# Loop tables copied by ScalarE at the outset, the small steps of three batch norm chunks moved to GpSimd, ten rooms for fetched images

## The chip, the cores and the metric

The kernel runs on one core of a Trainium2 chip. Its time is the device time of one execution in microseconds (us). The core has five engines that run their own instruction queues and wait for each other through semaphores: TensorE (PE, matrix products), VectorE (DVE), ScalarE (ACT), GpSimd (POOL) and SyncE (SP, which here only issues DMA transfers). Within a queue, instructions start in the order in which they stand.

## The reference

The input x has 128 images of 128 channels of 16x16 pixels. The reference does two layers.

```python
x = x + _L0_conv_ref(_gn(x), ...)            # group norm, batch norm, 4-bit activations, conv, batch norm, conv
t = _to_tokens(x)
t = t + _L1_attn_ref(_ln_t(t), ...)          # two Mamba-like scans, forward and backward
t = t + _L1_ffn_ref(_ln_t(t), ...)           # top-2 of 8 experts
x = _from_tokens(t, x)
```

What matters here is the first layer. The group norm takes the mean and variance of each image over groups of 4 channels; the batch norm takes the mean and variance of each channel over all 128 images of what the group norm returned. So nothing can be convolved before the last image has been read:

```python
def _bn(x, gamma, beta):
    m = jnp.mean(x, axis=(0, 2, 3), keepdims=True)
    v = jnp.var(x, axis=(0, 2, 3), keepdims=True)
    return (x - m) * jax.lax.rsqrt(v + EPS) * gamma[None, :, None, None] + beta[None, :, None, None]

h = _act_quant(_bn(x, gamma1, beta1))
out = _conv3x3(h, _weight_quant(w1) * pat1)
out = _act_quant(_bn(out, gamma2, beta2))
out = _conv3x3(out, _weight_quant(w2) * pat2) + x
```

## The kernel before

Channels lie on the 128 partitions; two images (128x512 values) are the unit of work, 64 units in all. There are four stages.

**Outset.** SP issues the 64 loads of the units (`xr`, line 371), then some 40 loads of the weights of the second layer (`load_weights`, lines 278 to 307), then the load of the second conv's weights (`w2`, line 401). DVE takes mean and variance of most images with `bn_stats` (line 443); every fourth image, up to `cuts[3]`, is summed by ACT in two passes, `Copy` (line 441) and `Square` (line 457). The images are worked in four chunks of 48, 48, 24 and 8. After the sums of a chunk come its small steps, on arrays of 128 partitions by as many columns as the chunk has images: mean and variance from the two halves, the mean over 4 channels by a matrix product with `grp`, the same for the variance, `1/sqrt`, one Newton step, and the products that the batch norm needs (`normed`, lines 420 to 434). Before the change `1/sqrt` is a `Sqrt` on ACT (line 481) and a reciprocal on DVE (line 424), and nearly all the small steps are DVE's, placed between its `bn_stats`. Between them DVE and ACT also prepare the first conv's weights (`conv_weights`, lines 148 to 185). At the end DVE folds the four chunks into a scale and an offset for each image (lines 495 to 511: `sc1`, `bi1`).

The outset also builds two constant tables for the main loop, `rows0` and `cols0` (128x2048 in bf16 each): POOL copies them together in `patterns` (lines 376 to 397), from two small selectors `heads` and `triple` that POOL also builds (lines 94 to 108), and SP stores them to HBM (`rows_d`, `cols_d`, lines 489 and 490), from where the main loop's `constants` loads them. Before the change these two stores stand last in SP's queue, behind the weight loads.

**First conv.** For each unit: ACT or POOL applies scale and offset (`q`, lines 525 and 527), DVE quantises into a padded buffer (`hpad`, line 192), PE does five products (`cv`, line 218), ACT adds an offset and copies the result out (`o1`, line 541), DVE takes its statistics (line 542), SP stores it to HBM (line 544), except for the first 8 units, which are kept (`kept`). The buffers of this stage lie where the outset's had been (the pool `setup1`), so its first instructions also wait until those buffers are free.

**Second conv.** For each unit: SP fetches the stored unit (`fetch`, line 618), ACT applies the second batch norm (line 622), DVE quantises, PE convolves, POOL or ACT scales x (lines 663 and 665), DVE adds (line 666), PE transposes (`yt_ps`, line 631), ACT copies it out (`yt`, line 633), SP stores it (`y_d`, line 635). Fetched units have 6 buffers, and the program asks for unit i+5 at unit i. The order in which the instructions of all these stages stand in the five queues is set by a scheduler when the kernel is built, from its own estimate of durations.

**Main loop** (from about 294 us on). The second layer, 64 units in an order written out by hand (`T`, a table of places, `manual_schedule`). It holds most of the time and the change does not touch it.

GpSimd's power instruction is used for `1/sqrt` in several places already: lines 133 (1 column), 557 (1), 595 (4) and 1060 (8), where `mhalf` holds -0.5.

Of the kernel before, what the change touches and what calls it, by code (L numbers as in the profile page):

```python
# [8 lines left out]
F32 = mybir.dt.float32  # L9
BF16 = mybir.dt.bfloat16  # L10
AF = mybir.ActivationFunctionType
ALU = mybir.AluOpType
AX = mybir.AxisListType

P = 128
NT = 256
EPS = 1e-5
# [4 lines left out]
NH = 4  # L22
HD = 64
# [11 lines left out]
def kernel(ctx: ExitStack, tc: tile.TileContext, a: dict):  # L35

    nc = tc.nc
    x_d, out_d = a["x"], a["out"]
    B = x_d.shape[0]
    NP = B // 2  # L40
# [19 lines left out]
    rows_d = dram.tile([P, NH, 2, 2, P], BF16, name="rows_d")  # L60
    cols_d = dram.tile([P, 2, 2, 2, 2, P], BF16, name="cols_d")

    ident = const.tile([P, P], F32, name="ident")
    make_identity(nc, ident)
    ones = const.tile([P, P], F32, name="ones")
# [30 lines left out]
    nc.gpsimd.memset(heads, 0.0)  # L96
    nc.gpsimd.memset(triple, 0.0)
    for m in range(2):
        for q in range(3):
            for t in (3 + 4 * q, 15 + 4 * q):  # L100
                nc.gpsimd.affine_select(
                    out=heads, in_=heads, pattern=[[-1, NH]], compare_op=ALU.not_equal,
                    fill=-1.0, base=-(64 + 32 * m + t), channel_multiplier=1,
                )
            nc.gpsimd.affine_select(
                out=triple[:, m : m + 1], in_=triple[:, m : m + 1], pattern=[[0, 1]], compare_op=ALU.not_equal,
                fill=1.0, base=-(64 + 32 * m + q), channel_multiplier=1,
            )
# [235 lines left out]
    with tc.tile_pool(name="w1p", bufs=1) as w1p:  # L344

        grp = w1p.tile([P, P], F32, name="grp")
        nc.gpsimd.affine_select(
            out=grp, in_=ones, pattern=[[-4, 32], [0, 4]], compare_op=ALU.is_ge, fill=0.0,
            base=0, channel_multiplier=1,
        )  # L350
        nc.gpsimd.affine_select(
            out=grp, in_=grp, pattern=[[4, 32], [0, 4]], compare_op=ALU.is_ge, fill=0.0,
            base=3, channel_multiplier=-1,
        )
        nc.vector.tensor_scalar(grp, grp, 0.25, None, ALU.mult)
# [4 lines left out]
        with tc.tile_pool(name="setup1", bufs=1) as setup, tc.tile_pool(  # L360
            name="psa", bufs=1, space=PSUM
        ) as psa:
            w1 = w1p.tile([P, 9, P], F32, name="w1", tag="w")
# [5 lines left out]

            for i in range(NP):  # L370
                nc.sync.dma_start(xr[i], x_c[:, 2 * i : 2 * i + 2, :])
            rows0 = setup.tile([P, NH, 2, 2, P], BF16, name="rows0")
            cols0 = setup.tile([P, 2, 2, 2, 2, P], BF16, name="cols0")
            far = setup.tile([HD, 1], BF16, name="far")

            def patterns():
                nc.gpsimd.memset(far, -1e30)
                for h in range(NH):
                    nc.gpsimd.tensor_copy(
                        rows0[:, h].rearrange("p d t l -> p (d t l)"), heads[:, h : h + 1].to_broadcast([P, 4 * P])  # L380
                    )
                    nc.gpsimd.tensor_copy(
                        rows0[0:HD, h].rearrange("p d t (f l) -> p (d t f) l", l=HD),
                        ident[0:HD, 0:HD].unsqueeze(1).to_broadcast([HD, 2 * 2 * 2, HD]),
                    )
                for m in range(2):
                    for d in range(2):
                        sign = 1 - 2 * d
                        nc.gpsimd.tensor_copy(
                            cols0[:, m, d].rearrange("p j f l -> p (j f l)"), triple[:, m : m + 1].to_broadcast([P, 4 * P])  # L390
                        )
                        for half in range(2):
                            nc.gpsimd.affine_select(
                                out=cols0[0:HD, m, d, :, half, :], in_=far.unsqueeze(2).to_broadcast([HD, 2, P]),
                                pattern=[[0, 2], [sign, P]], compare_op=ALU.is_ge, fill=0.0,
                                base=-sign * HD * half - 1, channel_multiplier=-sign,
                            )

            load_weights()
            w2 = w1p.tile([P, 9, P], F32, name="w2", tag="w")  # L400
            nc.sync.dma_start(w2, a["L0_conv_w2"])

# [11 lines left out]
            cuts = [0, 3 * B // 8, 3 * B // 4, B - max(B // 16, 1), B]  # L414
# [5 lines left out]
            def normed(c):  # L420

                of = slice(cuts[c], cuts[c + 1])
                var_, gm_, dev_, ga_, qv_, dm_ = (t[:, of] for t in (var, gm, dev, ga, qv, dm))
                nc.vector.reciprocal(ga_, ga_)
                nc.vector.tensor_tensor(dm_, ga_, ga_, ALU.mult)
                nc.vector.tensor_tensor(dm_, dm_, qv_, ALU.mult)
                nc.vector.tensor_scalar(dm_, dm_, -0.5, 1.5, ALU.mult, ALU.add)
                nc.vector.tensor_tensor(ga_, ga_, dm_, ALU.mult)
                nc.vector.scalar_tensor_tensor(shift[:, of], gm_, -1.0, ga_, ALU.mult, ALU.mult)
                nc.gpsimd.tensor_scalar(ares[:, of], ga_, 1.0, SCALE, ALU.add, ALU.mult)  # L430
                nc.gpsimd.tensor_scalar(bres[:, of], shift[:, of], SCALE, None, ALU.mult)
                nc.vector.tensor_tensor(dev_, dev_, ga_, ALU.mult)
                nc.vector.tensor_tensor(var_, var_, ga_, ALU.mult)
                nc.vector.tensor_tensor(var_, var_, ga_, ALU.mult)

            for c in range(4):
                of = slice(cuts[c], cuts[c + 1])
                for b in range(B)[of]:
                    x_b = xr[b // 2][:, b % 2, :]
                    if by_scalar(b):  # L440
                        nc.scalar.activation(junk, x_b, AF.Copy, accum_out=bst[:, b, 1:2])
                    else:
                        behind = nc.vector.bn_stats(bst[:, b, :], x_b)
                if c > 0:

                    with tc.issue_after(behind.ins):
                        normed(c - 1)
                mean_, var_, dm_, gm_, dev_, qv_, ga_ = (t[:, of] for t in (mean, var, dm, gm, dev, qv, ga))
                mine = [b for b in range(B)[of] if by_scalar(b)]
                if mine:  # L450

                    picked = slice(mine[0], cuts[c + 1], 4)
                    nc.vector.tensor_scalar(neg[:, picked], bst[:, picked, 1], -1.0 / NT, None, ALU.mult)
                    nc.vector.tensor_scalar(bst[:, picked, 1], neg[:, picked], -1.0, None, ALU.mult)
                    nc.vector.tensor_scalar(bst[:, picked, 4], neg[:, picked], -1.0, None, ALU.mult)
                    for b in mine:
                        nc.scalar.activation(
                            junk, xr[b // 2][:, b % 2, :], AF.Square, bias=neg[:, b : b + 1],
                            accum_out=bst[:, b, 2:3],
                        )  # L460

                nc.vector.tensor_tensor(mean_, bst[:, of, 1], bst[:, of, 4], ALU.add)
                nc.vector.tensor_scalar(mean_, mean_, 0.5, None, ALU.mult)
                nc.vector.tensor_tensor(dm_, bst[:, of, 1], bst[:, of, 4], ALU.subtract)
                nc.vector.tensor_tensor(dm_, dm_, dm_, ALU.mult)
                nc.vector.tensor_tensor(var_, bst[:, of, 2], bst[:, of, 5], ALU.add)
                nc.vector.tensor_scalar(dm_, dm_, 0.25, None, ALU.mult)
                nc.vector.scalar_tensor_tensor(var_, var_, 1.0 / NT, dm_, ALU.mult, ALU.add)
# [4 lines left out]
                nc.vector.tensor_copy(gm_, gm_ps)  # L473
                nc.vector.tensor_tensor(dev_, mean_, gm_, ALU.subtract)
                nc.vector.tensor_tensor(qv_, dev_, dev_, ALU.mult)
                nc.vector.tensor_tensor(qv_, qv_, var_, ALU.add)
# [3 lines left out]
                nc.vector.tensor_scalar(qv_, gv_ps, EPS, None, ALU.add)  # L480
                nc.scalar.activation(ga_, qv_, AF.Sqrt)
# [3 lines left out]
                if c == 1:  # L485
                    for _ in weights:
                        pass
                    patterns()
                    nc.sync.dma_start(rows_d, rows0)
                    nc.sync.dma_start(cols_d, cols0)  # L490
                if c == 3:
                    normed(c)
# [112 lines left out]
    def conv2(taps, nq):  # L605
        with tc.tile_pool(name="pc", bufs=6) as pc, tc.tile_pool(
# [8 lines left out]
            def fetch(i):  # L615
                if NP > i and i not in kept:
                    qs[i] = pc.tile([P, 2, NT], F32, name=f"q2_{i}", tag="q")
                    nc.sync.dma_start(qs[i], o1_d[i])
# [30 lines left out]
            for i in range(5):  # L649
                fetch(i)  # L650
            for i in range(3):
                quantised(i)
            for i in range(NP):
                b = 2 * i
                fetch(i + 5)
# [656 lines left out]
```

## Time and profile before

| | us |
|---|---|
| median of 3 runs (2553.06 to 2555.53) | 2554.39 |
| the profiled execution, its own time | 2554.94 |
| its span, first to last instruction | 2553.1 |
| last unit of x issued by SP | 51.4 |
| scale and offset of the first conv ready (`bi1`) | 77.6 |
| first `q` of the first conv on ACT | 85.7 |
| first product of the first conv on PE | 87.3 |
| first product of the second conv on PE | 174.7 |
| last `xr` sum of the second conv on DVE | 292.2 |

| engine | busy us | share of the span |
|---|---|---|
| PE | 2415.3 | 95% |
| DVE | 2253.2 | 88% |
| ACT | 2173.0 | 85% |
| POOL | 1629.3 | 64% |

The shares are means over all four stages. The change lies in the first 294 us, so the rows to read are those of that stretch: there PE is idle for the first 87 us, POOL is nearly idle from 20 to 87 us, and DVE is busy 98% of the time from 20 to 60 us.

### The profile page before, as it was taken

To read this page: it belongs to the slowest core of one execution; us is meant where nothing else is said; L and a number is where in the kernel's file an instruction comes from. 1 tells how busy PE (TensorE), PEld (TensorE's weight loads), DVE (VectorE), ACT (ScalarE), POOL (GpSimd) and SP (SyncE) were. 2 spreads that over 40 slices of the span, in tenths; PEclk is the share of its full clock that TensorE was granted. 3 is DMA by queue.
4 is the path that set the end of the run, shared out by engine and by line. 5 is a ranking of instruction groups with operands and counts; after the bars stand their busy time and mean duration, and the time that the engine had idled before them with its cause. 6 is when DMAs were issued, how large, how long until landed. Compare 5 with 4: busy or idle time off the path is not lost.

```text
span 2553.1 us, 49290 instructions
## 1 busy us (share of the span) xinstructions
PE 2415.3 (95%) x15940; PEld 1479.9 (58%) x15940; DVE 2253.2 (88%) x6163; ACT 2173.0 (85%) x4455; POOL 1629.3 (64%) x1694
## 2 busy tenths in 40 slices
PE   0688889999999999999999999999999999999997
PEld 0235456666666666666666666666666666666663
DVE  8787699999999999999999999999999999999883
ACT  5678699888889998889898888998988899898881
POOL 3468026676666666666666666666667666666666
PEclk9999899999999999999999999999999999999998
DMA  9358633434444444444444344444433443443343
GB/s 287 124 192 281 227 67 110 125 111 123 130 124 122 122 125 118 120 132 128 120 126 124 114 119 129 128 121 119 129 118 117 132 132 121 123 123 116 107 125 107
DMA packets 302167, 339.58 MB, mean 133 GB/s; under 512 B 56768, under 2 KB 226752, under 8 KB 301888
## 3 DMA queue, kind: packets, MB, share of 16 engines
q1 hardware_dynamic: 301888, 336.21, 43.3%
q8 instruction: 133, 2.18, 0.3%
q14 instruction: 146, 1.20, 0.2%
HBM read 262.72 MB, written 56.62 MB: 125 GB/s over the span
## 4 chain that ended last, share of the span: by engine, by line
PE 88%; DMA 4%; DVE 3%; ACT 2%; issue 1%; SPq 1%; POOL 1%; POOLq 0%; ACTq 0%; DVEq 0%
PE f_ps L1189 17%; PE x_ps L877 13%; PE y_ps L1012 10%; PE z_ps L920 9%; PE o_ps L1072 9%; PE sg L965 5%; PE xt_ps L932 4%; PE y_ps L1018 4%; PE g_ps L951 4%; PE cv L218 4%; DMA xr<-in_x 2%; PE n_ps L1045 1%; PE u_ps L1094 1%; PE f_ps L1184 1%; PE u_ps L750 1%
## 5 line engine op out<-in xcount | busy, mean ns | idle before, releaser
L1177 POOL TENSOR_TENSOR gb<-gb,u2T 128x512 f32<-128x512 f32 x512 | 641.3, 1277 | 122.7 <-PE y_ps L1018 68.8
L895 DVE SCALAR_TENSOR_TENSOR xc<-x_ps,cw,xc 128x510 f32<-128x510 f32 (+2 forms) x768 | 571.7, 744 | 46.5 <-ACT xc L889 36.9
L1028 POOL TENSOR_TENSOR yg<-yg,z 128x512 f32<-128x512 f32 x256 | 325.9, 1279 | 352.1 <-DVE yg L1024 155.1
L1189 PE MATMUL f_ps<-gb,ew 128*128 128x512 f32 x1024 | 510.1, 602 | 6.7 <-POOL gb L1177 6.4
L877 PE MATMUL x_ps<-uT,wx 128*128 128x512 f32 x768 | 402.9, 607 | 7.6 <-ACT e L731 3.3
L731 ACT ACTIVATE e<-sg 128x512 f32<-128x512 f32 x512 | 299.3, 591 | 49.9 <-PE sg L965 44.4
L731 ACT ACTIVATE e<-e,ends 128x128 f32<-128x128 f32 x1024 | 325.0, 392 | 0.0
L1012 PE MATMUL y_ps<-e,xt 128*64 128x256 f32 x2048 | 317.8, 389 | 0.2 <-DVE yg L1024 0.2
L993 DVE TENSOR_TENSOR e<-e,g_ps 128x1024 f32<-128x1024 f32 x256 | 311.6, 1217 | 5.5 <-ACT e L731 2.4
L895 DVE SCALAR_TENSOR_TENSOR bc<-x_ps,cw,bc 128x510 f32<-128x510 f32 (+2 forms) x384 | 286.7, 747 | 20.5 <-ACT bc L889 4.1
L1189 PEld LDWEIGHTS f_ps<-gb,ew 128*128 128x128 f32 x1024 | 180.5, 192 | 174.2 <-issue 136.2
L920 PE MATMUL z_ps<-uT,wz 128*128 128x512 f32 x512 | 271.2, 611 | 1.5 <-ACT xc L889 1.0
L889 ACT ACTIVATE xc<-x_ps,cb,cw 128x512 f32<-128x512 f32 x256 | 199.0, 777 | 64.0 <-PE x_ps L877 57.4
L1072 PE MATMUL o_ps<-wo,yg 128*128 128x128 f32 x2048 | 251.4, 276 | 0.2 <-DVE e L998 0.2
L1072 PEld LDWEIGHTS o_ps<-wo,yg 128*128 128x128 f32 x2048 | 240.5, 193 | 11.1 <-DVE g L1149 8.4
L1024 DVE SCALAR_TENSOR_TENSOR yg<-xc,dcol,y_ps 128x512 f32<-128x512 f32 x256 | 189.8, 742 | 50.1 <-PE y_ps L1018 46.8
L1060 POOL TENSOR_TENSOR rr<-rr,mhalf 128x8 f32<-128x8 f32 x64 | 109.9, 1718 | 161.7 <-DVE g L1151 82.7
L1018 PE MATMUL y_ps<-e,xt 128*64 128x128 f32 x2048 | 199.0, 273 | 0.0
L965 PE MATMUL sg<-rows,cols 128*128 128x256 bf16 x1024 | 192.1, 274 | 5.8 <-ACT e L731 2.8
L1018 PEld LDWEIGHTS y_ps<-e,xt 128*64 128x64 f32 x2048 | 147.0, 137 | 74.1 <-DVE e L998 0.5
L218 PE MATMUL cv<-hpad,wq 128*128 128x512 bf16 x640 | 161.7, 396 | 19.5 <-DVE hpad L192 19.4
L1012 PEld LDWEIGHTS y_ps<-e,xt 128*64 128x64 f32 x2048 | 118.9, 136 | 100.9 <-issue 53.8
(256 smaller groups left out, 4813.9 us busy)
## 6 DMA issues: line engine op xcount, KB each, us to landing
gb<-gd SPq DMA_DIRECT2D x256, 512.0 KB
e<-cum SPq DMA_DIRECT2D x256, 256.0 KB
xr<-in_x SPq DMA_DIRECT2D x64, 256.0 KB
cc<-bc SPq DMA_DIRECT2D x128, 128.0 KB
out<-ob SPq DMA_DIRECT2D x64, 256.0 KB
y<-yt SPq DMA_DIRECT2D x60, 256.0 KB
yt<-y SPq DMA_DIRECT2D x60, 256.0 KB
o<-o SPq DMA_DIRECT2D x56, 256.0 KB
```

The source lines that it names most:

```text
L731: nc.scalar.activation(out, in_, func, **more)
L877: nc.tensor.matmul(ps, wx[d][:, n * P : (n + 1) * P], uTs[i], start=True, stop=True)
L895: nc.vector.scalar_tensor_tensor(acc[:, :, to], raw[:, :, of], cw[:, d, n, 3 - back : 4 - back], acc[:, :, to], ALU.mult, ALU.add,)
L920: nc.tensor.matmul(ps, wz[:, d, n * P : (n + 1) * P], uTs[i], start=True, stop=True)
L965: nc.tensor.matmul(sg[:, :, of], c_[:, k, d, s, half, :], r_[:, :, d, s, of], start=True, stop=True)
L993: nc.vector.tensor_tensor(e0.rearrange("p h t l -> p h (t l)"), e0.rearrange("p h t l -> p h (t l)"), gps[i, d, k][:, 0:NT].unsqueeze(1).t ...
L1012: nc.tensor.matmul(y_ps[64 * q : 64 * q + 64, k, :], xt[:, 2 * k + s0, 64 * h : 64 * h + 64], e0[:, h].rearrange("p t l -> p (t l)"), star ...
L1018: nc.tensor.matmul(y_ps[64 * q : 64 * q + 64, k, s1 * P : (s1 + 1) * P], xt[:, 2 * k + s1, 64 * h : 64 * h + 64], e1[:, h, :], start=False ...
L1028: large(nc.gpsimd.tensor_tensor(yg, yg, zs[i, d][:, n, :], ALU.mult))
L1072: nc.tensor.matmul(o_ps[:, (2 * j + d) * P : (2 * j + d + 1) * P], ygs[i, d, n][:, t * P : (t + 1) * P], wo[d][:, n, :], start=(n == 0), s ...
L1177: large(nc.gpsimd.tensor_tensor(gb[:, e], gb[:, e], u2Ts[i], ALU.mult))
L1189: nc.tensor.matmul(f_ps, ew[:, e, :], gbs[i, e], start=False, stop=(e == NE - 1))
```

## The change

Three groups of edits.

1. `heads` and `triple` come from three DVE instructions on the identity matrix in place of 18 selections on POOL. `patterns` runs on ACT before the statistics: three copies of 64x2048 and eight of 64x256, from a table `far` that POOL makes with two selections. The two stores to HBM stand in SP's queue after 32 of the 64 loads of x. The load of `w2` stands right behind the loads of x, ahead of the weight loads. The factor 0.25 on `grp` moves from DVE to POOL.
2. The chunks become 48, 48, 16 and 16 images. The small steps of the first three go to POOL, with the copies out of PSUM on ACT; those of the fourth stay on DVE. `Sqrt` and reciprocal are replaced in all four by POOL's power instruction. `normed` follows its own chunk directly (it used to be issued behind the next chunk's `bn_stats`), and its fused steps are split in two.
3. Fetched units of the second conv get 10 buffers in place of 6, and the program asks for unit i+8 in place of i+5.

```diff
-    for m in range(2):
-        for q in range(3):
-            for t in (3 + 4 * q, 15 + 4 * q):
-                nc.gpsimd.affine_select(out=heads, ...)
-            nc.gpsimd.affine_select(out=triple[:, m : m + 1], ...)
+    strips = ident[:, HD:].rearrange("p (m r) -> p m r", r=32)
+    nc.vector.tensor_reduce(heads, strips[:, :, 3:27].rearrange("p m (u h) -> p h m u", h=NH), AX.XY, ALU.add)
+    nc.vector.tensor_scalar(heads, heads, -1.0, None, ALU.mult)
+    nc.vector.tensor_reduce(triple, strips[:, :, 0:3], AX.X, ALU.add)
...
-        nc.vector.tensor_scalar(grp, grp, 0.25, None, ALU.mult)
+            nc.gpsimd.tensor_scalar(grp, grp, 0.25, None, ALU.mult)
...
+            def patterns():
+                nc.scalar.copy(rows0[HD:]..., heads[HD:]...to_broadcast([HD, NH, 4 * P]))
+                nc.scalar.copy(rows0[:HD]..., ident[:HD, :HD]...to_broadcast([HD, 8 * NH, HD]))
+                nc.scalar.copy(cols0[HD:]..., triple[HD:]...to_broadcast([HD, 2, 8 * P]))
+                for d in range(2):
+                    for half in range(2):
+                        for m in range(2):
+                            nc.scalar.copy(cols0[:HD, m, d, :, half, :], far[...]...to_broadcast([HD, 2, P]))
+
+            patterns()
             for i in range(NP):
                 nc.sync.dma_start(xr[i], x_c[:, 2 * i : 2 * i + 2, :])
-            load_weights()
+                if i == NP // 2:
+                    nc.sync.dma_start(rows_d, rows0)
+                    nc.sync.dma_start(cols_d, cols0)
             w2 = w1p.tile([P, 9, P], F32, name="w2", tag="w")
             nc.sync.dma_start(w2, a["L0_conv_w2"])
+            load_weights()
...
-            cuts = [0, 3 * B // 8, 3 * B // 4, B - max(B // 16, 1), B]
+            cuts = [0, 3 * B // 8, 3 * B // 4, 7 * B // 8, B]
...
             def normed(c):
-                nc.vector.reciprocal(ga_, ga_)
-                nc.vector.tensor_tensor(dm_, ga_, ga_, ALU.mult)
-                nc.vector.tensor_tensor(dm_, dm_, qv_, ALU.mult)
-                nc.vector.tensor_scalar(dm_, dm_, -0.5, 1.5, ALU.mult, ALU.add)
-                nc.vector.tensor_tensor(ga_, ga_, dm_, ALU.mult)
-                nc.vector.scalar_tensor_tensor(shift[:, of], gm_, -1.0, ga_, ALU.mult, ALU.mult)
+                eng = nc.vector if c == 3 else nc.gpsimd
+                eng.tensor_tensor(dm_, ga_, ga_, ALU.mult)
+                eng.tensor_tensor(dm_, dm_, qv_, ALU.mult)
+                eng.tensor_scalar(dm_, dm_, -0.5, 1.5, ALU.mult, ALU.add)
+                eng.tensor_tensor(ga_, ga_, dm_, ALU.mult)
+                eng.tensor_tensor(dev_, dev_, ga_, ALU.mult)
+                eng.tensor_tensor(var_, var_, ga_, ALU.mult)
+                eng.tensor_tensor(var_, var_, ga_, ALU.mult)
+                eng.tensor_tensor(tmp_, gm_, ga_, ALU.mult)
+                eng.tensor_scalar(shift[:, of], tmp_, -1.0, None, ALU.mult)
                 nc.gpsimd.tensor_scalar(ares[:, of], ga_, 1.0, SCALE, ALU.add, ALU.mult)
                 nc.gpsimd.tensor_scalar(bres[:, of], shift[:, of], SCALE, None, ALU.mult)
...
-                if c > 0:
-                    with tc.issue_after(behind.ins):
-                        normed(c - 1)
...
-                    nc.vector.tensor_scalar(neg[:, picked], bst[:, picked, 1], -1.0 / NT, None, ALU.mult)
+                    nc.gpsimd.tensor_scalar(neg[:, picked], bst[:, picked, 1], -1.0 / NT, None, ALU.mult)
...
-                nc.vector.tensor_copy(gm_, gm_ps)
+                if c == 3:
+                    nc.vector.tensor_copy(gm_, gm_ps)
+                else:
+                    nc.scalar.copy(gm_, gm_ps)
...
-                nc.vector.tensor_scalar(qv_, gv_ps, EPS, None, ALU.add)
-                nc.scalar.activation(ga_, qv_, AF.Sqrt)
+                if c == 3:
+                    nc.vector.tensor_scalar(qv_, gv_ps, EPS, None, ALU.add)
+                else:
+                    nc.scalar.activation(qv_, gv_ps, AF.Identity, bias=epsc)
+                nc.gpsimd.tensor_tensor(ga_, qv_, mhalf[:, 0:1].to_broadcast([P, n]), ALU.pow)
...
+                normed(c)
...
-                    qs[i] = pc.tile([P, 2, NT], F32, name=f"q2_{i}", tag="q")
+                    qs[i] = pc.tile([P, 2, NT], F32, name=f"q2_{i}", tag="q", bufs=10)
...
-            for i in range(5):
+            for i in range(8):
                 fetch(i)
...
-                fetch(i + 5)
+                fetch(i + 8)
```

In the built order of the changed kernel, POOL's queue holds the small steps of chunk 0, then those of chunk 1, then those of chunk 2, then the power instruction of chunk 3; nothing of a later chunk stands ahead of the end of an earlier one, but for three steps of chunk 2 among the last five of chunk 1. DVE's queue holds all its `bn_stats` and weight steps first and the small steps of chunk 3 last. ACT's queue holds the tables right behind the `Tanh` of the first weights.

## The prediction

> **What bounds the kernel now.** I read the core's span first (2553.1 us, granted clock 0.991), then the chain of waits up to 300 us, the timelines of DVE, ACT, POOL and SP over the first 95 us, the power instruction's rows, and the waits of the second conv. The main loop (from 294 us) keeps its instructions and their order, so the sum below is a shift of its start.
>
> The chain of waits at the end of the outset (start, us, what):
>
> ```profile
> 77.09 1.19 SPq L303
> 78.32 0.59 SPq L307
> 79.03 0.67 SPq L401
> 79.74 5.88 DMA rows_d<-rows
> 85.72 1.10 ACT q L525 x2
> 86.85 0.44 DVE hpad L192
> 87.33 4.28 PE cv L218 x10
> ```
>
> DVE's timeline there:
>
> ```profile
> 77.33 0.29 DVE L511 TENSOR_SCALAR bi<-bi,b 128x128 f32<-128x128 f32 x1
> 85.75 0.16 DVE L211 TENSOR_SCALAR less<-less_ps 128x1 f32<-128x1 f32 x1 [8.13 <-DMA rows_d<-rows]
> ```
>
> Scale and offset are ready at 77.62, yet the first conv starts at 85.72: its buffers lie where `rows0` lay, and the store of `rows0` stands behind the weight loads in SP's queue. 8.1 us are lost to a store. Until then DVE is the bound: 98% busy from 20 to 60 us, its last `bn_stats` starting at 68.5, though the last unit of x was issued at 51.0 and lands some 6 us later.
>
> The power instruction on POOL, by columns (min/median/max ns):
>
> ```profile
> L133 POOL TENSOR_TENSOR rs<-rs,mhalf x1: 582/582/582, 75.9 to 75.9; 128x1 f32<-128x1 f32 x1
> ...
> L595 POOL TENSOR_TENSOR rstdb<-rstdb,mhalf x64: 1006/1007/1008, 370.0 to 2515.8; 128x4 f32<-128x4 f32 x64
> ...
> L1060 POOL TENSOR_TENSOR rr<-rr,mhalf x64: 1635/1637/1807, 363.8 to 2508.2; 128x8 f32<-128x8 f32 x64
> ```
>
> 142 ns per column from 1 to 4, 157 from 4 to 8: no sign that it gets cheaper. The same chain shows POOL's small steps when each needs the one before:
>
> ```profile
> 369.98 1.01 POOL L595 TENSOR_TENSOR rstdb<-rstdb,mhalf 128x4 f32<-128x4 f32 x1 [4.42 <-DVE rstdb L592]
> 371.07 0.20 POOL L596 TENSOR_TENSOR nmrb<-mvb,rstdb 128x4 f32<-128x4 f32 x1
> 371.36 0.23 POOL L597 TENSOR_SCALAR nmrb<-nmrb 128x4 f32<-128x4 f32 x1
> ```
>
> One such step comes 0.29 us after the other at 4 columns. The 128x512 product takes 1.28, so 2.1 ns per column: 0.38 at 48 columns, 0.32 at 16; steps that need not wait for each other start some 0.12 sooner. I take 0.35 and 0.30 as means.
>
> **The change part by part.**
>
> *Tables.* On ACT behind `Tanh` (ends 9.84): a 128x1152 cast takes 1.15, so 2048 columns about 1.9; three of these and eight of 0.33 make 8.3, ready at 18.1. SP wants them after 32 loads, at about 28: no wait. ACT's first sums start 8 us late and have caught up with the loads by 22.5. The two stores delay the last 32 units of x by 2.6 us (`rows_d` and `cols_d` released their waiters at 85.72 and 87.06, 1.3 apart): last unit at 59.7, DVE's last `bn_stats` at about 60.4. The wait of 8.1 us goes. `w2` passes the weight loads, which then end at about 82; their first reader is the second conv, at 204. DVE loses the 7.84 us that `grp` took at 11.14 to 18.98, while POOL was busy with casts until 18.9. None of this is on the path any more, as what follows shows.
>
> *Small steps on POOL.* I follow the queues in their built order.
> - Chunk 0: ACT's last sum ends at 27.2 (unit 23 lands at 26.7). Twelve `Square` at 0.635 (7.6), three weight casts at 1.07 (3.2) and 2.3 of waits for POOL's steps and its weight difference (2.36): 40.3. Four steps on POOL (1.45), a product (0.66), a copy (0.26) and hand-overs: 42.8. Power at 48 columns, 1.637 + 40 x 0.157 = 7.9: 50.7. Eleven steps, 3.8: 54.5.
> - Chunk 1: only now can POOL make `neg` (0.3), though its images were summed at 48. Twelve `Square` and 0.9 of waiting for the mean: 63.4. 2.5 as before: 65.9. Power: 73.8. Nine steps: 76.8.
> - Chunk 2 (16): `neg`, four `Square`, 2 us of POOL's steps for the mean: 81.6. Four steps, product, copy: 83.8. Power, 1.637 + 8 x 0.157 = 2.9: 86.7. Eleven steps at 0.29: 89.9.
> - Chunk 3: DVE has waited since 61; the power of its 16 columns is last in POOL's queue: 92.8. Four dependent DVE steps (0.2 each) and the products: 94.0. From the reduce of `dev` (73.66 before) to `bi1` (77.62) it took 3.96: 98.0.
>
> Power alone is 7.9 + 7.9 + 2.9 + 2.9 = 21.6 us of this path; in the kernel before it is `Sqrt` and reciprocal, 0.24 and 0.45, mostly beside other work. Behind 98.0, DVE enters the first conv's code with nothing to hide it: the same passage into the second conv took 1.85 us (171.36 to 173.21). With `less` (0.16) and `hpad` (0.45) PE starts at 100.5 against 87.33: **+13.2 us**.
>
> The bounds of the power at 48 columns: 1.64 us (the row at 8, if a long one cost no more) and 7.9; were it 1.64 throughout, the same walk ends at 82.9 and PE starts at 85.4, -1.9. I take 7.9, since both slopes agree. For the 57 small steps: 0.1 less or more each is 5.7 us either way.
>
> A rule that speaks against this part: DVE does the 48-column steps in 0.18 to 0.24 us each, POOL needs 0.38 by the rows above. The Trainium skill (GPSIMD Engine Reference, Engine selection) says to keep elementwise work on VectorE, GpSimd being about two times slower on two inputs; at twice DVE's roughly 0.12 us spacing the 57 steps would cost 0.24 each, 5 us less than in my sum. It has no price for a power.
>
> *First conv.* Without `Sqrt` the table is never changed: the load at 94.66 (1.28 us, in the chain of waits) goes, and so does the one at 48.19. PE had 42 products in 90 to 100 us against 45 later, so it was hardly held up. Between 0 and -1.3: **-0.6**.
>
> *Ten buffers.*
>
> ```profile
> ACT q L622 <- DMA q<-o: 13.7, 16, 1.5
> PEld yt_ps L631 <- ACT yt L633: 9.6, 13, 1.2
> ```
>
> ACT waits 13.7 us for fetches, 16 times; PE then waits for ACT's copies. If all of it went, PE would win about 8 us. But the built order spends the buffers elsewhere: the scheduler also moves ACT's reading of a unit ahead. Unit 20 is now asked for 7 copies ahead of its use in place of 3, unit 30 4 in place of 2, but units 50 and 60 still 2. A fetch takes 3 to 5 us and a unit 1.55, so only the first half gains: 7.7 of the 13.7 us lie before 240 us, and PE loses about 0.4 to 0.6 of what ACT waits. Between 0 and -8: **-3**.
>
> Sum: 13.2 - 0.6 - 3.0 = +9.6 on the span, 2562.7; the profiled run was 2554.94, so 2564.5, and 0.55 less beside the median of 2554.39: **2564 us**.
>
> **The rivals.**
> - *The power is cheap when long* (ends on the other side): start of the first conv -1.9, in all -5.5, 2549. For it: no row is longer than 8 columns. Against it: the slope rises rather than falls. It decides from 0.078 us per column down, half the measured slope: there the sum is zero.
> - *Prefetch does all it could*: -8 in place of -3, 2559. For it: the 13.7 us. Against it: the order of the second half.
> - *POOL's steps are dearer* beside DVE's `bn_stats`: the scaling of 48 columns (L430) took 0.61 at 54.91 and 0.25 at 65.86. 0.1 more each: 2570. Against: DVE has nothing to do from 61 on, where half of the path lies.
> - *Power half as dear* (0.08 to 0.1 per column): 2554 to 2557.
>
> **How the numbers follow.** Main case 0.62 (2560 to 2569), dear steps 0.15 (2569 to 2576), full prefetch 0.10 (2556 to 2560), cheap power 0.08 (2546 to 2552), half-priced 0.05. 0.2% is 5.1 us, about what a measurement of this kernel can tell from no change: 2549.3 to 2559.5. Slower: 0.62 + 0.15 + 0.03 = 0.80; same: 0.07 + 0.05 + 0.01 = 0.13; faster 0.07. The range takes in the prefetch and half-priced cases and most of the dear steps: 2554 to 2573; the main case's own is 2560 to 2569.
>
> **What would show it.** The two long powers at 7.9 us and the two of 16 columns at 2.9; POOL's chain unbroken from about 41 to 93 us; DVE idle from 61 with only a few steps until 93; the first `q` at about 98, with `rows_d` no longer its releaser; no table load at 48 or 95; in the second conv, fewer waits for fetches before 250 us and as many after. I am wrong if the long powers take under 4 us, if the first conv starts before 90 us, or if the second conv shrinks by more than 8.

## The result, and the profile after

The changed kernel takes 2566.18 us (median of 6 runs, 2564.44 to 2568.68) against 2555.22 for the kernel before on the same chip (6 runs, 2553.06 to 2558.03): a ratio of 1.0043, 95% interval 1.0030 to 1.0056, so 11 us slower. The forecast was 2564 us, and slower.

| from the two profiled executions, us | before | after | difference | forecast |
|---|---|---|---|---|
| scale and offset ready (end of `bi`) | 77.62 | 98.44 | +20.8 | +20.4 (98.0) |
| from there to the first product of the first conv | 9.71 | 3.84 | -5.9 | -7.2 |
| first product of the first conv | 87.33 | 102.28 | +14.95 | +13.2 |
| first conv, to the second conv's first product | 87.41 | 87.10 | -0.3 | -0.6 |
| second conv, to the start of its last sum of x | 116.72 | 113.49 | -3.2 | -3.0 |
| the rest | 2261.64 | 2262.43 | +0.8 | 0 |
| span | 2553.1 | 2565.3 | +12.2 | +9.6 |

The chain of waits at the end of the outset, where before the store of `rows_d` stood (start, us, what):

```profile
66.58 8.05 POOL ga L487
...
84.49 2.94 POOL ga L487
...
90.41 2.90 POOL ga L487
...
98.15 0.30 DVE bi L513
98.45 0.26 DVEq L216
...
98.85 2.81 issue
...
102.28 3.14 PE cv L209 x7
```

Line 487 is the power instruction. It stands three times in the last 36 us, and nothing that waits for a store is left. Between `bi` and the first product stands "issue", time in which DVE waits for nothing that the profile shows, behind the branch into the conv's code (`DVEq L216`).

POOL's timeline (start, duration, what; in brackets the idle time before it):

```profile
43.19 8.04 POOL L487 TENSOR_TENSOR ga<-qv,mhalf 128x48 f32<-128x48 f32 x1 [1.13 <-ACT qv L486]
...
54.53 0.33 POOL L436 TENSOR_SCALAR bres<-shift 128x48 f32<-128x48 f32 x1
54.94 0.27 POOL L452 TENSOR_SCALAR neg<-bst 128x12 f32<-128x12 f32 x1
...
66.58 8.04 POOL L487 TENSOR_TENSOR ga<-qv,mhalf 128x48 f32<-128x48 f32 x1 [1.13 <-ACT qv L486]
...
84.49 2.93 POOL L487 TENSOR_TENSOR ga<-qv,mhalf 128x16 f32<-128x16 f32 x1 [1.05 <-ACT qv L486]
...
90.37 2.93 POOL L487 TENSOR_TENSOR ga<-qv,mhalf 128x16 f32<-128x16 f32 x1
```

The forecast ends of the four powers were 50.7, 73.8, 86.7 and 92.8 us; they came at 51.2, 74.6, 87.4 and 93.3. The step `neg` of chunk 1 (line 452) starts at 54.94, right behind chunk 0's last step: this is what ACT waits for before its `Square` sums of chunk 1. ACT's timeline there, and its waits from 20 to 104 us (us in total, times, longest):

```profile
55.24 0.51 ACT L456 ACTIVATE junk<-xr,neg 128x256 f32<-128x256 f32 x1 [6.87 <-POOL neg L452]
```

```profile
ACT junk L456 <- POOL neg L452: 17.2, 2, 10.3
```

And DVE, which was the bound before, stands still for 30.5 us in two waits between 61 and 93.3 us. The first is for chunk 3's product, which stands behind chunk 2's last product in PE's queue, and that one waits for POOL; the second is for chunk 3's power:

```profile
84.57 0.17 DVE L474 COPY gm<-gm_ps 128x16 f32<-128x16 f32 x1 [23.48 <-PE gm_ps L472]
...
93.34 0.18 DVE L426 TENSOR_TENSOR dm<-ga 128x16 f32<-128x16 f32 x1 [7.03 <-POOL ga L487]
```

ACT's waits in the second conv (160 to 310 us), before:

```profile
ACT q L622 <- DMA q<-o: 13.7, 16, 1.5
ACT yt L633 <- PE yt_ps L631: 8.2, 9, 2.3
...
ACT yt L633 <- DMA y<-yt: 0.3, 1, 0.3
```

and after:

```profile
ACT yt L635 <- PE yt_ps L633: 13.5, 15, 1.4
ACT q L624 <- DMA q<-o: 5.6, 8, 1.3
...
ACT yt L635 <- DMA y<-yt: 2.0, 4, 0.9
```

The waits for fetches fell from 13.7 us to 5.6, those for PE's transposes rose from 8.2 to 13.5, and those for the stores of `yt` from 0.3 to 2.0. ACT waits nearly as long as before, but for something else. Split in the middle of the stage, the number of waits for fetches goes from 9 to 2 in the first half (7.7 us to 1.4) and from 7 to 6 in the second (5.9 us to 4.2).

### The profile page after: what moved, and what is told of

The parts are those of the page before. It is cut to its first block, busy times and chain, and to the rows that moved or that the text cites. A ratio compares the mean times of both kernels' runs of the same rounds, so it can differ in the third digit from the quotient of the medians.

```text
span 2565.3 us, 49244 instructions
## 1 busy us (share of the span) xinstructions
PE 2413.8 (94%) x15940; PEld 1482.5 (58%) x15940; DVE 2238.7 (87%) x6096; ACT 2177.1 (85%) x4458; POOL 1659.5 (65%) x1731
## 4 chain that ended last, share of the span: by engine, by line
PE 89%; DMA 3%; DVE 3%; ACT 2%; POOL 2%; issue 1%; SPq 0%; POOLq 0%; DVEq 0%; ACTq 0%
PE f_ps L1191 17%; PE x_ps L879 13%; PE y_ps L1014 9%; PE z_ps L922 9%; PE o_ps L1074 9%; PE sg L967 5%; PE xt_ps L934 4%; PE cv L209 4%; PE y_ps L1020 4%; PE g_ps L953 4%; DMA xr<-in_x 2%; PE n_ps L1047 1%; PE u_ps L1096 1%; PE f_ps L1186 1%; PE u_ps L752 1%
## 5 line engine op out<-in xcount | busy, mean ns | idle before, releaser
L209 PE MATMUL cv<-hpad,wq 128*128 128x512 bf16 x640 | 162.4, 399 | 20.1 <-DVE hpad L183 20.1
```

## The experiments

The theory: the power instruction of POOL lies on the path that ends the outset, nearly all of its 21.9 us; the rest of the change is a gain. The rivals: the many small steps on POOL cost the time and the power lies beside other work; early chunks have slack; the tables and stores are worth little. "First product" is PE's first of the first conv, 87.33 before and 102.28 after; it has hardly any scatter (four executions of the changed outset gave 102.19 to 102.57), so it tells more than the times.

**The power back to Sqrt and reciprocal.** The changed kernel, with

```diff
-                nc.gpsimd.tensor_tensor(ga_, qv_, mhalf[:, 0:1].to_broadcast([P, n]), ALU.pow)
+                nc.scalar.activation(ga_, qv_, AF.Sqrt)
+                nc.vector.reciprocal(ga_, ga_)
```

> The changed kernel with one edit: the power instruction of the four chunks goes back to Sqrt on ACT and a reciprocal on DVE; the small steps stay on POOL. Theory (the power instruction lies on the path that ends the outset, 8.04 + 8.04 + 2.93 + 2.93 us of it): the first product of the first conv moves from 102.28 us to about 87 (84 to 90; part of the 22 us comes back, since DVE now waits in its queue for two reciprocals), and the time falls by about 15 us to 2551. Rival (the long row of small steps on POOL costs the time, the power instruction lies beside other work): the first product stays above 97 us, 2561 or more.

```profile
82.19 19.57 PE L209 MATMUL cv<-hpad,wq 128*128 128x512 bf16 x75 [5.46 <-DVE hpad L183]
```

First product at 82.19 us, 20.1 earlier than in the changed kernel; ratio to the kernel before 0.9966 (0.9955 to 0.9978), 8.7 us faster. The theory stands: with this one line undone, the change that cost 11 us gains 9, with all other steps still on POOL. (Their order is not quite the same: the scheduler, which places every build anew, now sets the first steps of chunk 2 among the last ones of chunk 1. What that is worth by itself was not separated.) The expected start, 87 with a range of 84 to 90, was 5 us too late: I had let the reciprocals in DVE's queue cost more than they did. They do cost. DVE's waits from 20 to 84 us:

```profile
DVE ga L488 <- ACT ga L487: 14.5, 4, 5.4
```

**Chunk 0's power twice.** The changed kernel, with

```diff
                 nc.gpsimd.tensor_tensor(ga_, qv_, mhalf[:, 0:1].to_broadcast([P, n]), ALU.pow)
+                if c == 0:
+                    nc.gpsimd.tensor_tensor(ga_, qv_, mhalf[:, 0:1].to_broadcast([P, n]), ALU.pow)
```

> The changed kernel with the power instruction of chunk 0 (48 columns) issued twice in a row. Theory (POOL's work is one chain without slack from about 41 us on): the whole 8.1 us come out again at the end, first product of the first conv at 110.4 us, time 2574. Rival (chunk 0 is early enough to be hidden behind the loads and ACT's sums of chunk 1): under 3 us, 2569 or less.

POOL's timeline of this run:

```profile
42.97 8.04 POOL L487 TENSOR_TENSOR ga<-qv,mhalf 128x48 f32<-128x48 f32 x1 [1.13 <-ACT qv L486]
51.09 8.01 POOL L489 TENSOR_TENSOR ga<-qv,mhalf 128x48 f32<-128x48 f32 x1
59.17 0.27 POOL L426 TENSOR_TENSOR dm<-ga 128x48 f32<-128x48 f32 x1
```

And PE's:

```profile
110.20 2.29 PE L209 MATMUL cv<-hpad,wq 128*128 128x512 bf16 x5 [12.23 <-DVE hpad L183]
```

First product at 110.20: 7.9 of the added 8.1 us come out 50 us later. The ratio to the kernel before is 1.0087 (1.0070 to 1.0103), 22 us, where the changed kernel loses 11. So even the earliest power, which runs while x is still being loaded, has no slack behind it. That is the price of lengthening it. What taking it away can win is less than its 8.0 us: ACT waits 6.9 us for the `neg` behind it, and without the power (the run before this one) that `neg` starts at 49.56 in place of 54.94, 5.4 us earlier. The chain of waits of the changed kernel does not say so. For this stretch it gives

```profile
54.76 6.28 DMA w<-in_L_conv_w
...
61.47 2.23 DMA wx<-in_L_attn_fwd_in_proj
63.73 0.19 ACT junk L456
```

and jumps to loads that have nothing to do with ACT's sums at 63.73. Those sums began at 55.24, and what started them is the `neg` of POOL. The doubled instruction settles what the chain guessed wrongly.

**The power alone, in the kernel before.** The kernel before, with

```diff
-                nc.vector.reciprocal(ga_, ga_)
...
-                nc.scalar.activation(ga_, qv_, AF.Sqrt)
+                nc.gpsimd.tensor_tensor(ga_, qv_, mhalf[:, 0:1].to_broadcast([P, n]), ALU.pow)
```

> The kernel before with one edit: Sqrt and reciprocal replaced by POOL's power instruction, the small steps stay on DVE. The powers of the 48-column chunks take 8.0 us, that of 24 columns 4.2 and that of 8 columns 1.6 (from the changed kernel's rows). Theory (what is on the path is what DVE's queue waits for: chunk 0's power is hidden behind DVE's sums, those of chunks 1, 2 and 3 are not): DVE stands still for about 7 us behind the power of chunk 1 at 63 us, for 4 behind that of chunk 2 and for 1.6 behind that of chunk 3, bi is ready at about 90 in place of 77.6 us, and as the wait for the store then is hidden, the first product of the first conv comes at about 94 in place of 87.3, time about 6.5 us above the kernel before. Rival (in this arrangement POOL is idle and the powers lie beside DVE's sums): bi at 80 or earlier, first product at 87, time as before.

DVE's timeline of this run:

```profile
74.00 0.21 DVE L424 TENSOR_TENSOR dm<-ga 128x48 f32<-128x48 f32 x1 [7.50 <-POOL ga L480]
...
85.37 0.18 DVE L424 TENSOR_TENSOR dm<-ga 128x24 f32<-128x24 f32 x1 [3.97 <-POOL ga L480]
...
88.23 0.17 DVE L424 TENSOR_TENSOR dm<-ga 128x8 f32<-128x8 f32 x1 [1.24 <-POOL ga L480]
```

The three waits are there with about the sizes expected. `bi` is ready at 93.28 (expected 90) and the first product comes at 97.17 (expected 94), since chunk 0's power was not quite hidden either (2.6 us of waiting). Ratio 1.0025 (1.0014 to 1.0037), 6 us slower. The power costs on an idle POOL too, because DVE's queue waits for it in order. With the row of 24 columns its price is now known at six sizes: 0.58 us at 1 column, 1.01 at 4, 1.63 at 8, 2.93 at 16, 4.18 at 24, 8.04 at 48. From 8 columns on that is 0.16 us for each, a straight line.

**Where the small steps stand.** The changed kernel with Sqrt and reciprocal as in the first run, and

```diff
-                eng = nc.vector if c == 3 else nc.gpsimd
+                eng = nc.vector
```

> The changed kernel with the small steps of all chunks on DVE, and Sqrt on ACT with a reciprocal on DVE in place of the power instruction (the three neg steps stay on POOL). Against the run with Sqrt alone, whose first product of the first conv came at 82.19 us, this tells what the small steps on POOL cost when no power stands among them. Theory (about 6 us: POOL's steps are 0.3 us apart where DVE's are 0.1 to 0.2, and DVE no longer stands still for three reciprocals): first product at 76 us, as in the run with the tables alone (76.27), time about 15 us below the kernel before. Rival (the steps on POOL cost nothing once the power is gone, the difference came from the order of the weights): 82 us, time about 9 us below.

First product at 79.80, ratio 0.9951 (0.9934 to 0.9967). Against the 82.19 of the first run, the small steps on POOL cost 2.4 us, not the 6 expected. The other 3.5 us, down to the 76.27 of the tables alone (the next run), lie elsewhere. DVE's waits from 20 to some 80 us, here

```profile
DVE var L466 <- ACT junk L456: 4.1, 2, 2.2
...
DVE ga L488 <- ACT ga L487: 2.0, 3, 1.4
```

and in that next run, which has the chunks and the order of the kernel before

```profile
DVE var L464 <- ACT junk L455: 1.5, 2, 1.2
...
DVE ga L422 <- ACT ga L479: 0.3, 1, 0.3
```

4.3 us more of waiting: an order in which each chunk's steps follow its own sums lets DVE run into ACT's unfinished work, and the old one, with `normed` behind the next chunk's sums, mostly does not. The chunk sizes differ as well, so this is argued from the waits, not separated.

The Trainium skill (GPSIMD Engine Reference, Engine selection) calls GpSimd some two times slower than VectorE at two-input elementwise work. Here the same product at 48 columns takes 0.285 us on POOL and 0.20 on DVE, 1.4 times, and the whole row of steps cost 2.4 us. The rule points the right way, but the steps that it speaks of are the small part of the loss; the power is the large one.

**Tables and stores alone.** The kernel before with the first group of edits (the diff's parts on `heads`, `grp`, `far`, `patterns`, the two stores, `w2` and `load_weights`).

> The kernel before with only the first group of edits: tables copied by ACT at the outset, stores of the tables after 32 of the loads of x, weight loads behind the load of w2. Small steps, Sqrt, reciprocal and six buffers as before. Theory (without the power instruction on the path, both the wait for the store of the tables and DVE's 7.84 us behind the selector are won): DVE's last bn_stats starts at about 61 in place of 68.5 us, bi ready at about 70.5, first product of the first conv at about 74.5 in place of 87.3 (the way into the conv's code, 3.8 us in the changed kernel, is no longer hidden), time about 2542. Rival (only the wait for the store was worth anything, ACT's later sums hold DVE's steps up by as much as DVE wins): first product at 81, time about 2548.

First product at 76.27, ratio 0.9953 (0.9936 to 0.9969), and again 76.25 and 0.9957 (0.9941 to 0.9973) in a repeat: 11 to 12 us faster. The chain of waits:

```profile
71.75 0.30 DVE bi L506
...
72.47 3.18 issue
...
76.27 4.05 PE cv L209 x10
```

Expected were 70.5 for `bi` and 74.5 for the first product; they came at 72.04 and 76.27. `bi` is ready 5.6 us earlier than before. DVE's last `bn_stats` ends at 63.3 in place of 68.9, which fits the 7.84 us by which the factor on `grp` held DVE up before; no run separates it from the rest of the group. And the 8.1 us behind the store are gone, less the passage into the code that they had covered.

**The store alone.** The kernel before, with the weight loads moved behind the two stores and nothing else:

```diff
-            load_weights()
...
                     nc.sync.dma_start(cols_d, cols0)
+                    load_weights()
```

> The kernel before with the weight loads issued behind the two stores of the tables, and nothing else moved. Theory (the 8.1 us between bi and the first q are a wait for the store, and some 3.8 us of passage into the conv's code lie hidden under it): bi stays at about 77.6 us, the first product of the first conv comes at 81.4 in place of 87.3, time about 2548.5. Rival (the wait is for the buffers of the outset as such, or the weight loads collide with something later): first product at 87 as before, 2554.

```profile
77.31 0.30 DVE bi L511
...
78.02 3.30 issue
...
81.97 2.31 PE cv L218 x5
```

`bi` at 77.60, first product at 81.97, ratio 0.9968 (0.9955 to 0.9980). One line moved in one queue is worth 5.4 us at the first product; what remains of the 9.7 us between `bi` and the product is 4.4 us of passage, 3.3 of them "issue" in its chain of waits.

**Ten buffers.** The changed kernel with six buffers and `fetch(i + 5)`; the tables alone with ten buffers and `fetch(i + 8)`; and both pairs once more.

> The changed kernel with the second conv's fetched units back to 6 buffers and asked for at i+5. Theory (the ten buffers are worth what the two traces show between the first product of the second conv and its last sum of x, 116.7 against 113.5 us): the outset stays as in the changed kernel (first product of the first conv at about 102.3 us), the second conv takes 116.7 us again, ACT waits some 13 us for fetches, and the time is about 3.2 us above the changed kernel's, so 14 to 15 us above the kernel before. Rival (the second conv is shorter for another reason, such as the place of its weights' load or the chunks): it stays at 113.5, and the time at the changed kernel's 11 us above before.

> The kernel before with the first group of edits (tables, stores, order of SP's queue) and the ten buffers, without the second group. Theory (the two gains are in different stages and add): first product of the first conv at 76.3 us, second conv 113.5 us long, time 14 to 16 us below the kernel before. Rival (an earlier first conv or another order of ACT's queue takes the prefetch's gain away): second conv 116 us or more, time 12 us below, as with the tables alone.

> The changed kernel as it is (ten buffers), once more, beside the next run on the same chip. So far the second conv, from its first product to its last sum of x, took 113.5 us with ten buffers in the changed kernel and 114.5 with six, but 113.95 with six and 114.35 with ten behind the tables alone. If the ten buffers are worth 3 us, this run is 113 to 114 us long there and 3 us shorter than the next run in its time; if an execution's own scatter is as large as the gain, it lies anywhere between 113 and 116.

> The changed kernel with six buffers, once more. If the ten buffers are worth 3 us: second conv 116 to 117 us, time 3 us above the run before this one. If they are worth 1 us or less: second conv within the same 113 to 116 us as with ten, the times' intervals lie over each other.

> The kernel before with the tables alone (six buffers), once more, beside the next run on the same chip. If the ten buffers are worth 3 us: second conv 116 to 117 us. If they are worth 1 us or less: 113 to 115 as before, time about 12.5 us below the kernel before.

> The kernel before with the tables and the ten buffers, once more. If the ten buffers are worth 3 us: second conv 113 to 114 us, time 3 us below the run with the tables alone. If they are worth 1 us or less: both within the scatter, second conv 113 to 116, times' intervals over each other, about 13 us below the kernel before.

| second conv in us, one profiled execution each | six buffers | ten buffers |
|---|---|---|
| changed kernel | 114.52, 116.49 | 113.49, 115.40 |
| the tables alone | 113.95, 114.66 | 114.35, 110.98 |
| other runs (kernel before, store, power alone; Sqrt, power twice, steps on DVE) | 116.72, 118.70, 116.66 | 114.25, 116.11, 115.19 |
| mean of seven | 115.96 | 114.25 |
| ACT's waits for fetches | 12.0 to 15.7 | 5.4 to 10.1 |

The 3.2 us between the two first traces, close to the forecast, was luck. One execution differs from another of the same kernel by up to 3.4 us in this stage. The two means differ by 1.7 us, the two groups overlap, and by their scatter (1.7 us in each) the 95% interval of the difference is about -0.2 to 3.7: it takes in nothing at all as well as the 3 us forecast. The times don't part them either: changed kernel 1.0043 and 1.0054 with ten, 1.0051 and 1.0051 with six; tables 0.9942 and 0.9946 with ten, 0.9953 and 0.9957 with six, all within each other's intervals. What does move in every run are ACT's waits for fetches, by about 6 us in the mean; how much of that PE sees, this scatter does not tell.

The version with the first and third group of edits and without the second beats both kernels: 0.9942 (0.9925 to 0.9959) and 0.9946 (0.9932 to 0.9961), about 14 us below the kernel before and, by the ratios, 25 to 28 below the changed one.

## Why the prediction was right, point by point

- **The power is dear and on the path.** Right in size and place: 8.04 and 2.93 us for 7.9 and 2.9 forecast, and the run without it starts 20.1 us earlier. The two slopes of the rows at 1, 4 and 8 columns carried to 48. The rival of a cheap long power, and that of half its price, are out.
- **The walk through POOL's queue.** It ended at 98.0 where the trace has 98.44, and at every power on the way it was 0.5 to 0.8 us early, so this is no sum of large errors that cancel. The rival of dearer small steps is out: the eleven behind a power took 0.33 us each at 48 columns and 0.26 at 16 (51.31 to 54.94, 87.50 to 90.37), for 0.35 and 0.29 taken, and the loads of x didn't slow them.
- **The wait for `rows_d` goes.** Shown by the run with the store alone. That it is hidden by what follows was right: in the changed kernel its gain is spent.
- **The passage into the conv's code.** The term that was mis-sized: I took 1.85 us, from the second conv's entry, and 0.6 of DVE's work behind it, 2.5 together; it took 3.84 here and 3.85 to 4.75 in the twelve other runs in which no store covers it. That is 1.4 of the nearly 1.8 us by which the first product came late; the other 0.4 is the walk's.
- **First conv, -0.6.** -0.3 in the two traces. Over all executions, those without a change of ACT's table there took 86.76 us (mean of 6, 86.4 to 87.4), those with it 87.46 (mean of 8, 86.9 to 88.1): 0.7, about as forecast. The groups overlap and differ in more than the table (those without it are also the ones that start late), so this agrees with the forecast and does not test it.
- **Ten buffers, -3.** The mechanism was right (the first half gains, the second keeps its waits: 9 to 2 and 7 to 6), the size is not settled: 1.7 in the means, -0.2 to 3.7 with their scatter. Of the some 6 us that ACT waits less, 1.7 would be a quarter, where I took 0.4 to 0.6 for PE's share; that the first traces showed -3.2 was luck. The rival of a full prefetch, -8, is out.
- **The main loop at nothing.** +0.8 in the two traces; over 14 executions that stretch took 2260.4 to 2263.8, so this is scatter.
- **A slip in the rivals' prices.** The sum is not zero at 0.078 us per column. Four powers have 96 columns beyond the eighth, so by the walk's own terms the 9.6 us are gone at 0.057, and 0.08 to 0.1 per column give some 2556.6 to 2558.5, not 2554 to 2557. With 0.16 measured nothing hangs on it.

The sum was 2.6 us short on the span: 1.75 at the first product, the rest in the main loop and in the first conv, less 0.2 in the second.

## What to carry to other kernels

Before a step goes to an idle engine, price its dearest instruction at the size that it will have: two rows of the same instruction at smaller sizes were enough to see that one power would cost about as much as all of a chunk's other steps together. An idle engine that receives a chain of dependent steps becomes a queue, and a short step in it that another engine waits for (here `neg`) is late by everything that stands ahead of it. And where the chain of waits names a transfer that can't be the cause, double the suspected instruction and see where the time comes out.

## What was not expected of the hardware

- The passage into the first conv's code shows 2.8 to 3.7 us of "issue" on DVE behind the branch (lines 216 and 217 of the changed kernel). In the kernel before it was free, as the wait for a store covered it; in every version that removed or hid that wait it became visible, so removing a wait of 8.1 us was worth 5.4. The Trainium skill (Runtime: NRT & Kernel Launch, Instruction fetch mechanics) says that a taken branch to code outside the engine's window of instructions makes it fetch them by DMA first. The changed kernel's trace agrees so far that the only transfers between 97 and 104 us are 4 packets of an instruction queue. Whose instructions they carry it does not show, nor how long such a fetch takes, so that the passage is a fetch is not shown; why the second conv's entry took only 1.85 us stays open too.
- GpSimd's power costs 0.16 us for each column of 128 values, from 8 to 48 columns without a bend, where the product of the same shape on the same engine takes 0.285 us at 48 columns: 28 times.
- The second conv's length scatters by several us between executions of one kernel (110.98 and 114.35, 114.52 and 116.49), while the outset repeats to 0.5 us. A gain of 2 or 3 us in that stage can't be read from one pair of traces.
